# A power operation behind every second gather on GpSimd, from the eleventh row block to the end of a two-layer graph kernel

## The chip, the cores and the metric

The kernel runs on one core of a Trainium2 chip. The metric is the device time of one execution in microseconds, measured without a trace: the median of three runs. A traced execution of the same program gives the profile. In this text PE is TensorE, DVE is VectorE, ACT is ScalarE and POOL is GpSimd, as the profile names them.

## What is computed

The input is a node matrix `x` (2708 x 128, float32) and an adjacency matrix `adj` (2708 x 2708, float32), which is sparse: a row has its diagonal element and some neighbours, all with the same weight. Two layers follow each other. The first is a hyperbolic convolution with a dense product, the second a message layer whose inner sum runs over all pairs of nodes, but whose terms count only where `adj` isn't zero:

```python
# layer 0, in short: y from x and W, then
nominator = A_hat @ (gamma * XW)
denominator = _clamp_abs(A_hat @ (gamma - 1.0))
...
x = _layernorm(x + _L0_gnn_ref(x, adj, L0_gnn_W), axis=-1)
# layer 1
s = node_feats @ msg_w[:, :D].T
d = node_feats @ msg_w[:, D:].T
messages = gelu(s[:, None, :] + d[None, :, :] + msg_b)
aggregated = jnp.einsum('ijd,ij->id', messages, adj)
...
h = gelu(new_feats) + node_feats
x = _layernorm(x + layernorm(h) * ln_w + ln_b, axis=-1)
```

## The kernel before, in words

The 2708 rows are cut into 22 blocks of 128 (`NB`). For each block `b`, `layer0(b)` loads 1.4 MB of the transposed adjacency (`aT`, queue of SyncE), takes its sign on ScalarE (L364) and multiplies it with `y` on TensorE (L369). The same signs are used to find the edges: `keys` and `extract` encode the positions of nonzero elements, sort them with VectorE's top-8 instruction (L404) and place them, 128 edges to a tile, into 99 edge tiles for all blocks together. `TILES` gives the number of tiles of each of 25 lists; tile `t` belongs to one list and so to one block. For each tile there are `J[:, t]`, the column of each of its edges, and `F`, the flat address of the edge in `adj` (L500, L501).

GpSimd then runs two kinds of indirect DMA, both through the helper `gather` (L197):

- a V gather per tile, at the end of `extract`: it reads `adj` at the 128 addresses `F`. The values `V` are needed only in the check at the end (L848), which compares them with the weight of the row.
- a dd gather per tile, in `fetch`: it reads 128 rows of `table` (the product `d` of the second layer, written to memory by `layer0_end`, L583) at the rows `J`. The messages need these rows.

`fetch` issues up to four dd gathers, from block 14 on (`FETCH`) once per row block, later once in each call of `messages`, and fourteen times in a row at the end of layer 0. The rows go into a ring of `RING = 14` rooms of four tiles each. `messages` takes one room of up to four tiles: TensorE expands `s` for the edges (L736), VectorE builds the summing matrix `rv` (L738) and adds `dd` (L741), ScalarE takes the Gelu (L742), and TensorE sums over edges (L751). There are 26 such rooms: 24 of four tiles, one of two, one of one. When the last tile of a block is summed, `node` computes the update (L608 to L610) and the norms of its group (`finish`), and the result is stored.

GpSimd runs its instructions in the order in which they were issued, so V gathers, dd gathers and whatever else stands in its queue wait for one another. In `gather`, the argument `pause` puts a power operation on a tile of one column (`gap`, L202) into GpSimd's queue right behind the gather. It depends on nothing that changes and nothing reads its result. Before the change, V gathers of blocks below `PAUSED = 9` have it (61 of them) and no other gather.

Of the kernel before, what the change touches and what calls it, by code (L numbers as in the profile page):

```python
# [20 lines left out]
P = 128  # L21
# [7 lines left out]
CHUNKS = [(0, 10), (10, 20), (20, 22)]  # L29
PARTS = (0, 1, 2, 2)  # L30
GROUPS = [(0, 8), (8, 6), (14, 4), (18, 2), (20, 2)]
PAUSED = 9
EARLY = 8
FETCH = 14

# [3 lines left out]
SPLIT, BITS = 10, 16  # L39
# [42 lines left out]
def hyperbolic_then_message_kernel(  # L82
# [30 lines left out]
    w0_sb, wT, rowvec, o = pk[:, :D], pk[:, D : 5 * D].rearrange("p (i d) -> p i d", d=D), {}, 5 * D  # L113
# [55 lines left out]
    J = const.tile([P, NT], U32, name="J")  # L169
    V = const.tile([P, NT], F32, name="V")  # L170
# [25 lines left out]
    def gather(o, src, at, pause=False):  # L196
        last = nc.gpsimd.indirect_dma_start(  # L197
            out=o, out_offset=None, in_=src, in_offset=bass.IndirectOffsetOnAxis(ap=at, axis=0)
        )
        if pause:  # L200
            with tc.issue_after(last.ins), tc.high_priority():
                nc.gpsimd.tensor_tensor(gap, half, half, op=OP.pow)  # L202
# [10 lines left out]
    def flat(t):  # L213
        return t.rearrange("p b d -> p (b d)")
# [98 lines left out]
    for g, n in quads:  # L313
# [5 lines left out]
        t = small.tile([P, 4, D], F32, name="work", bufs=3)  # L319
        nc.vector.tensor_mul(t[:, :n, :], mx[:, g : g + n, :], mx[:, g : g + n, :])  # L320
        nc.vector.tensor_reduce(ss_m[:, g : g + n], t[:, :n, :], axis=AX.X, op=OP.add)
    for b in range(NB):
        t = small.tile([P, D], F32, name="junk")
# [89 lines left out]
    def extract(l):  # L413

        b, groups, c0, wa, wb, t0, n, late = LISTS[l]
# [34 lines left out]
        for k, _ in parts:  # L450
            first = n - late if k and wa else 0
            dl = deg[:, l, k + 1 : k + 2]
            for k0 in range(first, n, 4):
# [3 lines left out]
                o = flat(R[:, t0 + k0 : t0 + k1, :])  # L457
# [22 lines left out]
        F = small.tile([P, TMAX], U32, name="F", bufs=12)  # L480
        step = 512 // (C + 2)
        for k0 in range(0, n, step):
            k1 = min(n, k0 + step)
            w = k1 - k0
            t = slice(t0 + k0, t0 + k1)
# [16 lines left out]
                F[:, k0:k1], J[:, t], float(b * P * N - 1), rid[:, t], op0=OP.add, op1=OP.add  # L502
            )
        for t in range(t0, t0 + n):
            gather(V[:, t : t + 1], adj.rearrange("i (j o) -> (i j) o", o=1), F[:, t - t0 : t - t0 + 1], b < PAUSED)
        known[0] = b

    x1, x1T, gd = x_sb, xT, nom
# [183 lines left out]
    early, late, soon = {}, {}, set()  # L692
# [13 lines left out]
    rooms, sums, whole = [], {}, []  # L706
# [6 lines left out]
    def fetch():  # L713

        for _ in range(4):
            ready = [v for v in (True, False) if order[v] and order[v][0][0] < done[0] + RING]
            if not whole:
                ready = [v for v in ready if v and order[v][0][2] <= known[0]]
            if not ready:
                return  # L720
            q, k, _, t = order[min(ready, key=lambda v: order[v][0])].pop(0)
            while len(rooms) <= q:
                rooms.append(edge.tile([P, 4, P], F32, name="dd", bufs=RING))
            gather(rooms[q][:, k, :], table[: SPLIT * P] if t in soon else table, J[:, t : t + 1])

    def messages():

# [15 lines left out]
        for k, (b, t, first, final, before) in enumerate(ts):  # L743
# [12 lines left out]
            elif final:  # L756
                g0, gn = group[b]
                queue.append(node(gd[:, g0 : g0 + gn, :D], b - g0, b, g0, gn, [gd[:, b, :D]] if b < EARLY else []))
        fetch()
        step()  # L760
        step(1)
# [10 lines left out]
    with tc.issue_after(setup.ins):  # L772
        for b in range(NB):
            block = layer0(b)
            next(block)
            go_on(b, 0)
            for x in placed:
                next(x, None)
            placed = []
            next(block)  # L780
            go_on(b, 1)
            for x in found:
                next(x)
            placed, found = found, []
            sgn = next(block)
            for l in of_block[b]:
                keys(l, sgn)
                found.append(extract(l))
            if b == 0 or b == NB - 1:
                for x in found:  # L790
                    next(x)
                    next(x, None)
                for x in placed:
                    next(x, None)
                found, placed = [], []
            if b >= FETCH:
                fetch()
            for b0, b1 in CHUNKS:
                if b == b1 - 1 and b1 < NB:
                    ends.append((b1, layer0_end(b0, b1)))  # L800
                    next(ends[-1][1])
# [7 lines left out]
    for _ in range(RING):  # L809
        fetch()  # L810
# [25 lines left out]
    for i, v in enumerate(seconds):  # L836
        k = v.shape[1]
# [146 lines left out]
```

## Time and profile before

| | |
|---|---|
| time, median of 3 runs | 361.72 us (361.44 to 362.11) |
| traced execution | 472.48 us, span 470.8 us |
| gathers of either kind | 99 |
| power operations | 61, from 48.9 to 158.7 us |
| V gathers in the trace | first at 47.6 us, last at 310.0 us |
| dd gathers in the trace | first at 164.5 us, last at 403.2 us |

In the profile, a group's line gives source line, engine, operation, output and inputs, the count, then the busy time and the mean duration of one in ns, then the time that the engine was idle just before, and what ended most of that. A timeline's line gives start, length, engine, line and operation, and in brackets the idle time before it with what ended it. "remote", like "another core or an unknown queue", stands for a wait whose releaser isn't in the trace. "issue" is time in which the engine waited for nothing that the trace shows.

### The profile page before, as it was taken

To read this page: it belongs to the slowest core of one execution; us is meant where nothing else is said; L and a number is where in the kernel's file an instruction comes from. 1 tells how busy PE (TensorE), PEld (TensorE's weight loads), DVE (VectorE), ACT (ScalarE), POOL (GpSimd) and SP (SyncE) were. 2 spreads that over 40 slices of the span, in tenths; PEclk is the share of its full clock that TensorE was granted. 3 is DMA by queue.
4 is the path that set the end of the run, shared out by engine and by line. 5 is a ranking of instruction groups with operands and counts; after the bars stand their busy time and mean duration, and the time that the engine had idled before them with its cause. 6 is when DMAs were issued, how large, how long until landed. Compare 5 with 4: busy or idle time off the path is not lost.

```text
span 470.8 us, 8239 instructions
## 1 busy us (share of the span) xinstructions
PE 293.5 (62%) x2603; PEld 261.0 (55%) x2603; DVE 280.4 (60%) x1580; ACT 214.0 (45%) x609; POOL 242.4 (51%) x353
## 2 busy tenths in 40 slices
PE   4249999999999931252738947655300713999840
PEld 4139988999979820142627946544200712897730
DVE  0997998868979602022224779974000411799995
ACT  2953868786959802031324773932000201334441
POOL 6200888988888877735754400226776475200000
PEclk9758999999999965568957996859555665899865
DMA  8403544646644431122413300101211121100111
GB/s 335 207 1 124 194 179 135 236 142 230 222 172 158 161 117 37 28 79 95 151 28 141 126 1 24 34 11 45 52 50 50 30 54 36 24 1 4 43 37 43
DMA packets 16029, 45.15 MB, mean 96 GB/s; under 512 B 5418, under 2 KB 10942, under 8 KB 13166
## 3 DMA queue, kind: packets, MB, share of 16 engines
q1 hardware_dynamic: 9502, 37.43, 21.8%
q0 software_dynamic: 6336, 6.55, 5.6%
q10 hardware_dynamic: 144, 0.60, 0.4%
q8 instruction: 22, 0.36, 0.3%
q14 instruction: 25, 0.20, 0.1%
HBM read 41.74 MB, written 2.83 MB: 95 GB/s over the span
## 4 chain that ended last, share of the span: by engine, by line
PE 35%; DVE 27%; another core or an unknown queue 24%; ACT 6%; issue 5%; DMA 1%; DVEq 0%; ACTq 0%
PE mp L369 17%; PE kx L396 4%; PE mp L751 3%; DVE rv L738 2%; PE X L577 2%; DVE top L404 2%; PE sel L489 2%; DVE st L600 1%; PE X L736 1%; DMA xT<-in_x_t_dram 1%; DVE dd L741 1%; DVE nom L624 1%; PE kx L317 1%; PE sel L608 1%
## 5 line engine op out<-in xcount | busy, mean ns | idle before, releaser
L197 POOL DMA_INDIRECT V<-in_adj_dram,F x99 | 98.8, 998 | 108.5 <-DVE F L501 70.1
L369 PE MATMUL mp<-y,aT 128*128 128x130 f32 x968 | 141.7, 297 | 15.1 <-issue 14.8
L369 PEld LDWEIGHTS mp<-y,aT 128*128 128x128 f32 x968 | 127.1, 205 | 16.5 <-issue 16.3
L197 POOL DMA_INDIRECT dd<-table_dram,J x99 | 94.8, 958 | 47.8 <-issue 45.7
L364 ACT ACTIVATE sgn<-aT 128x2816 bf16<-128x2816 f32 x22 | 56.0, 2547 | 2.3 <-DMA aT<-in_adj_t_dram 2.1
L738 DVE TENSOR_SCALAR rv<-iotaN,rv_of 128x128 f32<-128x128 f32 x99 | 30.1, 347 | 42.8 <-PE X L736 34.2
L404 DVE MAX8 top<-kx 128x8 f32<-128x128 f32 (+3 forms) x133 | 25.3, 227 | 30.0 <-remote 25.4
L751 PE MATMUL mp<-rv,dd 128*128 128x128 f32 x198 | 35.7, 334 | 11.2 <-ACT dd L742 11.2
L489 PE MATMUL sel<-z,R 128*128 128x42 bf16 (+5 forms) x297 | 19.5, 194 | 31.6 <-issue 17.3
L202 POOL TENSOR_TENSOR gap<-gap 128x1 f32<-128x1 f32 x61 | 37.8, 620 | 1.5
L751 PEld LDWEIGHTS mp<-rv,dd 128*128 128x128 f32 x198 | 30.8, 236 | 13.4 <-ACT dd L742 12.1
L396 PE MATMUL kx<-kd,sgn 128*128 128x128 bf16 x484 | 32.9, 223 | 8.1 <-ACT sgn L364 8.1
L396 PEld LDWEIGHTS <-sgn 128*128 128x128 bf16 x484 | 28.1, 99 | 14.6 <-ACT sgn L364 8.5
L489 PEld LDWEIGHTS <-R 128*128 128x128 bf16 x297 | 15.2, 98 | 35.6 <-issue 19.6
L689 PE MATMUL mp<-ident,nom 128*128 128x128 f32 x44 | 10.0, 322 | 39.2 <-ACT nom L755 39.2
L494 DVE TENSOR_TENSOR work<-sel,place 128x120 f32<-128x120 f32 (+11 forms) x29 | 11.1, 382 | 37.4 <-remote 32.4
L742 ACT ACTIVATE dd<-dd 128x512 f32<-128x512 f32 (+2 forms) x26 | 15.8, 607 | 30.6 <-DVE dd L741 17.9
L456 ACT ACTIVATE away<-iota,mid 128x256 f16<-128x256 f32 (+3 forms) x54 | 28.7, 572 | 1.7 <-DVE mid L449 0.6
L689 PEld LDWEIGHTS mp<-ident,nom 128*128 128x128 f32 x44 | 7.1, 208 | 40.1 <-ACT nom L755 39.6
L736 PEld LDWEIGHTS <-R 128*128 128x128 bf16 x297 | 21.4, 108 | 12.4 <-issue 10.6
L755 ACT COPY nom<-mp 128x128 f32<-128x128 f32 x8 | 2.1, 262 | 46.8 <-remote 43.4
L408 ACT ACTIVATE junk_s<-kx 128x384 bf16<-128x384 f32 (+2 forms) x25 | 12.2, 486 | 18.2 <-DVE top L404 14.1
(224 smaller groups left out, 599.3 us busy)
## 6 DMA issues: line engine op xcount, KB each, us to landing
aT<-in_adj_t_dram SPq DMA_DIRECT2D x22, 1408.0 KB
V<-in_adj_dram,F POOLq DMA_INDIRECT x99
dd<-table_dram,J POOLq DMA_INDIRECT x99
xT<-in_x_t_dram SPq DMA_DIRECT2D x2, 704.0 KB
x_sb<-in_x_nm_dram SPq DMA_DIRECT2D x2, 704.0 KB
table_dram<-dt SPq DMA_DIRECT2D x4, 256.0 KB
out_dram<-nom SPq DMA_DIRECT2D x4, 256.0 KB
pk<-in_pack_dram ACTq DMA_DIRECT2D x1, 587.5 KB
```

The lines of the kernel that those rows point to most:

```text
L197: last = nc.gpsimd.indirect_dma_start(out=o, out_offset=None, in_=src, in_offset=bass.IndirectOffsetOnAxis(ap=at, axis=0))
L202: nc.gpsimd.tensor_tensor(gap, half, half, op=OP.pow)
L364: nc.scalar.activation(sgn, aT, AF.Sign, accum_out=signs[:, b : b + 1])
L369: p = nc.tensor.matmul(op[:, : D + 2], lhsT=aT[:, j, :], rhs=y[:, j, :], start=(j == 0), stop=(j == NB - 1))
L396: nc.tensor.matmul(kp[:, i * P : (i + 1) * P], lhsT=sgn[:, j, :], rhs=kd[:, q, :], start=False, stop=(i == len(groups) - 1 and j == j1 - 1),)
L404: nc.vector.max(top[:, c : c + 8], seg[:, s, :])
L456: nc.scalar.activation(r0, iota[:, k0 * P : k1 * P], AF.Abs, scale=2.0, bias=mid[:, k : k + 1])
L489: nc.tensor.matmul(sp[:, k, :], lhsT=R[:, t0 + k0 + k, :], rhs=z[:, i, :], start=(i == 0), stop=(i == 2))
L689: nc.tensor.matmul(ag[:, :P], lhsT=gd[:, b, :D], rhs=ident, start=True, stop=False)
L736: nc.tensor.matmul(X[:, k, :], lhsT=R[:, t, :], rhs=s3[:, b, i, :], start=(i == 0), stop=(i == 2))
L738: nc.vector.tensor_scalar(rv[:, k, :], iotaN, rid[:, t : t + 1], same[:, t : t + 1], op0=OP.is_equal, op1=OP.mult)
L751: nc.tensor.matmul(sums[b][:, :P], lhsT=dd[:, k, :], rhs=rv[:, k, :], start=(first and not mine), stop=final)
```

## The change

The power operation is to be spread over the rest of the gathers: all V gathers of blocks below 11 have it, from block 11 on every V gather of an odd tile, and of the dd gathers every one with odd `k`, the second and fourth of a room. It is for spacing the gathers that run back to back before the change, so that other engines have room between them.

```diff
-PAUSED = 9
 EARLY = 8
 FETCH = 14
...
         for t in range(t0, t0 + n):
-            gather(V[:, t : t + 1], adj.rearrange("i (j o) -> (i j) o", o=1), F[:, t - t0 : t - t0 + 1], b < PAUSED)
+            gather(V[:, t : t + 1], adj.rearrange("i (j o) -> (i j) o", o=1), F[:, t - t0 : t - t0 + 1], b < 11 or t % 2)
...
-            gather(rooms[q][:, k, :], table[: SPLIT * P] if t in soon else table, J[:, t : t + 1])
+            gather(rooms[q][:, k, :], table[: SPLIT * P] if t in soon else table, J[:, t : t + 1], k % 2)
```

## The prediction

> **What bounds the kernel now.** I read the times first, then the page's busy shares, its groups of instructions, then GpSimd's own timeline, the chain, and a table by stretch. The times already hold the main difficulty: 361.72 us is the median without a trace, while the traced execution took 472.48 us (span 470.8). The trace therefore holds about 110 us that the timed runs don't have, and the first job is to find which.
>
> ```profile
> PE 293.5 (62%) x2603; PEld 261.0 (55%) x2603; DVE 280.4 (60%) x1580; ACT 214.0 (45%) x609; POOL 242.4 (51%) x353
> PE 35%; DVE 27%; another core or an unknown queue 24%; ACT 6%; issue 5%; DMA 1%; DVEq 0%; ACTq 0%
> L197 POOL DMA_INDIRECT V<-in_adj_dram,F x99 | 98.8, 998 | 108.5 <-DVE F L501 70.1
> L197 POOL DMA_INDIRECT dd<-table_dram,J x99 | 94.8, 958 | 47.8 <-issue 45.7
> L202 POOL TENSOR_TENSOR gap<-gap 128x1 f32<-128x1 f32 x61 | 37.8, 620 | 1.5
> ```
>
> No engine is full, and 24% of the chain (113 us of 470.8) is a wait whose releaser the trace can't name. Without it the span would be 470.8 - 113 = 358 us, close to the untraced time. The stretches say where it sits (columns: window, length, then PE, PEld, DVE, ACT and POOL busy, clock, DMA share, GB/s):
>
> ```profile
> 125.00:150.00 25.00, 24.11 (x221) 21.25 (x219) 21.58 (x100) 19.52 (x55) 22.45 (x28) 1.00 0.50 169
> 180.00:200.00 20.00, 3.83 (x19) 2.85 (x19) 2.20 (x18) 3.04 (x11) 14.88 (x16) 0.50 0.11 30
> 340.00:360.00 20.00, 0.00 (x0) 0.00 (x0) 0.69 (x1) 0.00 (x0) 15.13 (x16) 0.50 0.20 52
> ```
>
> Up to 159 us every gather has its power operation and all engines are busy. After it gathers run back to back, and there the other engines nearly stop, while GpSimd goes on at an even beat. GpSimd's timeline at the border shows both beats:
>
> ```profile
> 157.66 0.99 POOL L197 DMA_INDIRECT V<-in_adj_dram,F  x1 [0.17 <-issue]
> 158.68 0.59 POOL L202 TENSOR_TENSOR gap<-gap 128x1 f32<-128x1 f32 x1
> 159.44 0.99 POOL L197 DMA_INDIRECT V<-in_adj_dram,F  x1 [0.17 <-DVE z L474]
> 160.74 0.96 POOL L197 DMA_INDIRECT V<-in_adj_dram,F  x1 [0.30 <-issue]
> 162.00 0.95 POOL L197 DMA_INDIRECT V<-in_adj_dram,F  x1 [0.30 <-issue]
> ...
> 360.44 0.95 POOL L197 DMA_INDIRECT dd<-table_dram,J  x1 [0.30 <-issue]
> 361.69 0.95 POOL L197 DMA_INDIRECT dd<-table_dram,J  x1 [0.30 <-issue]
> ```
>
> Start to start, a gather with its power operation takes 159.44 - 157.66 = 1.78 us, one without 162.00 - 160.74 = 1.26 us, and that 1.26 is the same at 361 us where nothing else runs. From 47.61 us (first gather) to 199.4 us GpSimd has no idle beyond these 0.2 to 0.3 us: it is behind with the V gathers and works off a queue.
>
> Now the timed run. If the unnamed waits are absent there, GpSimd's queue never empties: at 159.44 us it still has 38 V and 99 dd gathers, 137 in all, and 137 x 1.26 = 172.6 us, so the last gather ends at 332.0 us. Their inputs are in time: the row blocks pass at 7.35 us each (the sign activations before 159 us), so block 21's F would be there near 210 us, while the V gathers of blocks 17 to 21 stand behind 65 others in the queue (26 V, 39 dd) and come up at 241 us. After the last gather come its landing (2 us, below) and the last message with the final norms: from the last dd add at 448.34 us to the end at 470.77 that is 22.4 us. Sum 332.0 + 2 + 22.4 = 356.4, and 1.7 for what the time has over the span (472.48 - 470.8): 358.1 us. Measured is 361.72. So in the timed run I take the instruction stream of GpSimd as the path that sets the end, though the page shows it 51% busy. A second view agrees: with all data present, ten messages of four from 407.18 to 448.62 us (their Gelu starts) take 4.1 us each, and GpSimd delivers four gathers in 5.04 us, so the consumers wait for it.
>
> **What the Trainium skill says.** (1) Perfetto Trace Analysis, "GPSIMD Engine Instruction": reported spans of GpSimd are unreliable, and start-to-start spacing of consecutive instructions should be used. The trace agrees: a gather's span is 0.95 to 0.99 us, its spacing 1.26. (2) The same page, "DMA Instruction — SWDGE (GPSIMD)": the recorded end of such a gather is the end of descriptor writing, not of the data movement; so a gather occupies GpSimd for the whole 1.26 us, and landing comes on top. (3) DMA: Bandwidth & Descriptors, "Anatomy of one DMA — SWDGE (gpsimd) path", prices the fixed cost at about 2.0 us; the page's issue table gives no landing median for gathers, so I use it. (4) SBUF — State Buffer, "Who interferes with whom": a GpSimd instruction that reads SBUF and a VectorE one with two SBUF inputs hold a shared port in turn; TensorE and ScalarE wait for no one. The trace shows power operations stretched to 0.82 us at most (median 0.597), so this is small; and it can't explain the stops after 159 us, since TensorE and ScalarE stop too.
>
> **The change part by part.** The constant PAUSED goes: no cost. V gathers of blocks 9 and 10 (4 + 3) now all get the operation: 7 more. From block 11 on those with odd index (69 to 97): 15. Of the dd gathers those with k = 1 or 3: 24 full quads and one pair give 49. Together 71 power operations, 61 become 132. The order of the other four engines' instructions is unchanged; on GpSimd nine of the 71 end up behind another power operation instead of directly behind a gather, most in a row of seven just before the last 60 dd gathers.
>
> Price of one: 1.78 - 1.26 = 0.52 to 0.53 us between neighbours (0.59 to 0.60 of operation, the gap behind a gather 0.30 replaced by 0.03 + 0.17). Over the whole paused stretch (159.44 - 47.61) / 61 = 1.83 us a pair, so 0.57 with the stretched ones. Upper end: the longest operation, 0.82 + 0.17 - 0.27 = 0.72. I take 0.53, because the last 60 gathers run while VectorE is waiting, and little stretches them. 71 x 0.53 = 37.6 us (with 0.57: 40.5).
>
> What hides it? The operation reads and writes constants nobody waits for, but the gathers queued behind it wait, and behind those the dd adds (L741) and the last message. All 71 lie before the last gather. Were GpSimd ever idle in the timed run, that much would be hidden; my sum left 361.7 - 358.1 = 3.6 us unexplained, which is the most I find. So 361.7 + 37.6 = 399.3, less up to 3.6: 396 to 399, and I take 398. As a check, the floor by GpSimd alone is 332.0 + 37.6 + 2 + 22.4 + 1.7 = 395.7.
>
> **The rivals.**
> - Faster. The stops after 159 us exist in part in the timed run too, and the operation lets the other engines go on, as it does before 159 us. For it: the border is sharp, and no stop falls in the paused stretch. It needs gathers that cost less untraced, or GpSimd's floor forbids it. If the 0.30 us gap after a gather were only recording, a gather would cost 0.96: the last one before would end near 272 us, the run at 272 + 26 = 298, so 361.7 would hold 63 us of stops; after, the floor is 313 + 26 = 339 us. If the stops nearly vanish the time is about 345; if they only shrink with the count of gathers without the operation (137 to 66), 30 us stay and it is 369, slower again. Against it: the 1.26 sum meets 361.72 within 1%.
> - No change. GpSimd has slack in the timed run as in the trace (108.5 and 47.8 us idle before its gathers), the consumers set the end, and the operations fill that idle time: 361.7. Against it: those idle stretches follow the stops (6.9 us at 206, 29.5 at 300), and the consumers' 4.1 us per four is less than GpSimd's 5.04.
> - Partly hidden: GpSimd has about 15 to 20 us of slack, for instance waiting for the table's last rows before the final 60 dd gathers: 378 to 385.
> - Dearer: every operation at its stretched cost, 71 x 0.57 to 0.72: 402 to 413.
>
> **How the numbers follow.** Full cost on GpSimd's path (396 to 403) 0.60, dearer 0.04, partly hidden 0.11, no change 0.03, faster 0.22. Slower is 0.75, same 0.03, faster 0.22. The range starts at 354, which takes in no change and the near part of the faster case, and ends at 407, which takes in 0.57 with some to spare; outside stay about 0.16 of faster and 0.03 of dearer.
>
> **What would show it.** In the changed kernel's profile: 132 power operations; pairs at 1.78 and lone gathers at 1.26; the last dd gather about 38 us later than an unbroken queue would place it, with GpSimd's idle time before gathers nearly gone. I also expect the unnamed waits to shrink much, so that the traced span comes down towards the untraced time: if it falls while the untraced time rises, the stops belonged to tracing. I am wrong if gathers alternate in less than 3.04 us a pair (1.26 + 1.78), or if GpSimd has long idle times while VectorE or TensorE is full to the end, or if the untraced time falls below 361.

## The result, and the profile after

The changed kernel takes 400.24 us (median of 4 runs, 399.69 to 400.56), and the kernel before, run beside it, 361.92 us (361.44 to 363.2). The ratio is 1.1051, interval 1.1019 to 1.1083: 38.3 us slower. Ratios are taken from the fast runs alone, so a ratio can differ a little from the quotient of the two medians. The prediction was 398.0 us.

The page of the changed kernel: busy time of each engine, the chain by engine, the two kinds of gather and the power operation.

```profile
PE 282.8 (71%) x2603; PEld 255.0 (64%) x2603; DVE 281.3 (71%) x1580; ACT 213.2 (53%) x609; POOL 289.9 (73%) x424
PE 34%; DVE 22%; POOL 16%; DMA 12%; ACT 9%; issue 5%; DVEq 0%; POOLq 0%; ACTq 0%; SPq 0%
L196 POOL DMA_INDIRECT V<-in_adj_dram,F x99 | 100.1, 1012 | 52.0 <-DVE F L500 32.6
L196 POOL DMA_INDIRECT dd<-table_dram,J x99 | 97.2, 982 | 24.4 <-issue 22.1
L201 POOL TENSOR_TENSOR gap<-gap 128x1 f32<-128x1 f32 x132 | 81.6, 618 | 3.7
```

The 132 power operations are there. The wait on an unnamed releaser, 24% of the chain before, is gone from it, and GpSimd, which the chain before did not hold at all, has 16%. The traced execution took 400.42 us (span 398.7) and is one of the four runs behind the median, so the page shows what was timed. For the kernel before it took 472.48 us, far outside its runs.

GpSimd's timeline at the end of the gathers:

```profile
364.94 0.94 POOL L196 DMA_INDIRECT dd<-table_dram,J  x1 [0.30 <-issue]
365.91 0.58 POOL L201 TENSOR_TENSOR gap<-gap 128x1 f32<-128x1 f32 x1
366.67 0.99 POOL L196 DMA_INDIRECT dd<-table_dram,J  x1 [0.17 <-ACT agT L661]
367.97 0.95 POOL L196 DMA_INDIRECT dd<-table_dram,J  x1 [0.30 <-issue]
...
372.89 1.00 POOL L196 DMA_INDIRECT dd<-table_dram,J  x1 [0.17 <-issue]
```

Two gathers and one operation take 367.97 - 364.94 = 3.03 us start to start, against 1.78 + 1.26 = 3.04 before. The last gather ends at 373.89. From 159.97 us to there lie 137 gathers and 71 operations, and no idle time over 0.5 us between two of them.

The stretches (columns: window, length, PE, PEld, DVE, ACT and POOL busy, clock, DMA share, GB/s):

```profile
180.00:200.00 20.00, 20.00 (x225) 19.03 (x225) 16.21 (x111) 12.80 (x38) 15.75 (x19) 1.00 0.65 222
...
250.00:275.00 25.00, 3.77 (x47) 3.57 (x45) 0.69 (x1) 1.75 (x5) 21.13 (x28) 0.63 0.04 8
275.00:300.00 25.00, 15.51 (x135) 14.78 (x135) 13.11 (x43) 5.49 (x14) 20.91 (x27) 0.70 0.12 30
```

From 180 to 200 us, where the trace of before had TensorE busy for 3.83 of 20 us, it is full now. This is not yet the work of the operations: `e6_none` below has none and is full there too. From 250 to 275 us VectorE is busy for 0.69 us while GpSimd runs: there the others wait for the queue. VectorE stands in line behind the check of V, which needs the last V gather:

```profile
L847 DVE TENSOR_TENSOR work<-V,rv_of 128x99 f32<-128x99 f32 x1 | 0.3, 266 | 28.7 <-DMA V<-in_adj_dram,F 28.7
```

That wait of 28.7 us should cost little by itself, because the dd gathers that the messages need stand behind the same V gathers in GpSimd's queue; no run isolates it.

### The profile page after: what moved, and what is told of

It reads as the page before. It is cut to its first block, busy times and chain, and to the rows that moved or that the text cites. A ratio compares the mean times of both kernels' runs of the same rounds, so it can differ in the third digit from the quotient of the medians.

```text
span 398.7 us, 8310 instructions
## 1 busy us (share of the span) xinstructions
PE 282.8 (71%) x2603; PEld 255.0 (64%) x2603; DVE 281.3 (71%) x1580; ACT 213.2 (53%) x609; POOL 289.9 (73%) x424
## 4 chain that ended last, share of the span: by engine, by line
PE 34%; DVE 22%; POOL 16%; DMA 12%; ACT 9%; issue 5%; DVEq 0%; POOLq 0%; ACTq 0%; SPq 0%
PE mp L368 17%; POOL dd L196 8%; DMA aT<-in_adj_t_dram 8%; POOL gap L201 4%; PE kx L395 4%; POOL V L196 3%; DMA dd<-table_dram,J 3%; ACT sgn L363 3%; PE X L576 3%; PE sel L488 2%; PE mp L750 2%; DMA xT<-in_x_t_dram 1%; ACT nom L639 1%; PE kx L316 1%; DVE dd L740 1%
## 5 line engine op out<-in xcount | busy, mean ns | idle before, releaser
L196 POOL DMA_INDIRECT V<-in_adj_dram,F x99 | 100.1, 1012 | 52.0 <-DVE F L500 32.6
L368 PE MATMUL mp<-y,aT 128*128 128x130 f32 x968 | 128.9, 284 | 0.5 <-DMA aT<-in_adj_t_dram 0.5
L368 PEld LDWEIGHTS mp<-y,aT 128*128 128x128 f32 x968 | 117.6, 194 | 1.5 <-DMA aT<-in_adj_t_dram 0.8
L196 POOL DMA_INDIRECT dd<-table_dram,J x99 | 97.2, 982 | 24.4 <-issue 22.1
L201 POOL TENSOR_TENSOR gap<-gap 128x1 f32<-128x1 f32 x132 | 81.6, 618 | 3.7
L750 PE MATMUL mp<-rv,dd 128*128 128x128 f32 x198 | 37.9, 348 | 17.2 <-ACT dd L741 17.2
L750 PEld LDWEIGHTS mp<-rv,dd 128*128 128x128 f32 x198 | 32.4, 246 | 20.2 <-ACT dd L741 19.6
L735 PE MATMUL X<-s,R 128*128 128x128 bf16 x198 | 18.1, 240 | 30.1 <-DVE dd L740 30.1
L740 DVE TENSOR_TENSOR dd<-X,dd 128x512 f32<-128x512 f32 (+1 forms) x17 | 11.4, 671 | 19.0 <-DMA dd<-table_dram,J 18.8
L847 DVE TENSOR_TENSOR work<-V,rv_of 128x99 f32<-128x99 f32 x1 | 0.3, 266 | 28.7 <-DMA V<-in_adj_dram,F 28.7
L605 PE MATMUL sel<-pk,xT 128*128 128x128 f32 x44 | 11.7, 355 | 5.9 <-ACT nom L609 5.4
```

The costliest lines, as they stand in the source:

```text
L196: last = nc.gpsimd.indirect_dma_start(out=o, out_offset=None, in_=src, in_offset=bass.IndirectOffsetOnAxis(ap=at, axis=0))
L368: p = nc.tensor.matmul(op[:, : D + 2], lhsT=aT[:, j, :], rhs=y[:, j, :], start=(j == 0), stop=(j == NB - 1))
L735: nc.tensor.matmul(X[:, k, :], lhsT=R[:, t, :], rhs=s3[:, b, i, :], start=(i == 0), stop=(i == 2))
L750: nc.tensor.matmul(sums[b][:, :P], lhsT=dd[:, k, :], rhs=rv[:, k, :], start=(first and not mine), stop=final)
```

## The experiments

Two theories stood against each other. The queue: GpSimd's instruction stream sets the end, an operation costs about 0.53 us wherever it stands behind a gather after 159 us, and the stops in the trace of before belong to tracing. The stops: they are in the timed runs too, and operations between the gathers shrink them.

The runs fell on four chips, here A to D. The kernel before took 478.67 us on A (472.85 to 483.02), 363.49 on B, 363.01 on C and 363.25 on D. The lowest of its 23 times on A is as long as the traced 472.48 us, so on chip A the timed runs were as slow as the trace of before. Each result below is read against the kernel before on its own chip. Every chip was measured at one time only, so where a chip is named, a state that it was in at that time would fit as well. The chip of the first trace is not on record. In the experiments the traced execution is always one of the timed runs.

### No operation, on chip A and on chip B

`e1_none` and `e6_none` are one program, without any of the 61 operations that the kernel before has:

```diff
-gather(V[:, t : t + 1], ..., F[:, t - t0 : t - t0 + 1], b < PAUSED)
+gather(V[:, t : t + 1], ..., F[:, t - t0 : t - t0 + 1], False)
```

> No gather has a power operation: 61 fewer than before. Theory (GpSimd's queue sets the end, each operation costs it about 0.53 us, the stops belong to tracing): 32 us less on GpSimd up to 159 us, but in the changed kernel's trace the last rows of the table are stored only near 248 us, and the last 57 to 60 dd gathers need them: 248 + 60 x 1.26 + 26 + 2 = 352 us, so 345 to 352, faster than before; the traced span stays far above the time. Rival (in timed runs too, gathers that run back to back stop the other engines, and the operation relieves them): slower than before, 365 us or more.

On chip A: 514.39 us, ratio 1.0821 (1.0733 to 1.0908). It has fewer instructions on GpSimd and takes 36 us more. The rival had the direction, from a starting point of 362 us that did not hold on this chip.

> No power operation at all, as e1, for the other condition of the chip if this comparison lands in it. Where before is near 362: 345 to 352 by theory A (GpSimd's time is the path and the operations only cost). Where before is near 478: 514 as before.

On chip B: 355.2 us, ratio 0.9711 (0.9643 to 0.9779). It is faster, but by less than the 345 to 352 us expected. The chain by engine and one stretch, first for chip A, then for chip B, there with the stretch from 180 to 200 us as well:

```profile
PE 28%; another core or an unknown queue 28%; DVE 24%; issue 8%; ACT 7%; DMA 3%; POOL 0%; DVEq 0%; ACTq 0%; POOLq 0%; SPq 0%
200.00:220.00 20.00, 4.56 (x37) 3.92 (x35) 1.41 (x9) 2.18 (x5) 15.12 (x17) 0.74 0.21 66
```

```profile
PE 44%; DVE 24%; DMA 18%; ACT 7%; POOL 3%; issue 3%; DVEq 0%; POOLq 0%; SPq 0%; ACTq 0%
180.00:200.00 20.00, 20.00 (x217) 19.03 (x214) 15.67 (x103) 13.87 (x45) 15.31 (x16) 1.00 0.68 243
200.00:225.00 25.00, 16.52 (x132) 13.63 (x131) 23.17 (x143) 16.07 (x38) 19.21 (x20) 0.86 0.18 46
```

In these stretches the same program runs its gathers back to back on both chips. On A the other engines stop beside them (VectorE 1.41 of 20 us), on B they don't (23.17 of 25 us), and both runs were traced. So the trace does not make the stops, and gathers without an operation do not bring them on every chip.

The second reading is of size: 61 x 0.53 = 32 us were taken out on chip B and only 8.3 us came back. GpSimd's timeline there says why:

```profile
149.72 0.94 POOL L197 DMA_INDIRECT V<-in_adj_dram,F  x1 [23.53 <-DVE F L501]
...
157.38 0.97 POOL L197 DMA_INDIRECT dd<-table_dram,J  x1 [2.93 <-DMA table_dram<-dt]
158.65 0.94 POOL L197 DMA_INDIRECT V<-in_adj_dram,F  x1 [0.30 <-DVE top L404]
```

Without operations GpSimd catches up with VectorE, waits 23.53 us for addresses, then 2.93 us for the table. That makes 26.5 of the 32 us, so before about 157 us most of the operations' time is paid from this idle time, and only what comes after it counts in full. From 157.38 to 327.02 us there are 133 gathers and no further wait, 1.275 us each on the mean.

### Each half alone, on chip A

`e2_v_only` gives the V gathers their added operations and leaves the dd gathers without; `e3_dd_only` does the reverse.

```diff
 # e2_v_only: in the V gather
-b < PAUSED
+b < 11 or t % 2
 # e3_dd_only: in the dd gather
-J[:, t : t + 1])
+J[:, t : t + 1], k % 2)
```

> Only the V half of the change: 22 more operations than before, all ahead of the last 60 dd gathers. Theory: 22 x 0.53 = 11.7 us, so 373 to 374. If GpSimd waits for the table there and hides them: 362 to 365. If the dd half alone costs: 362.

> Only the dd half of the change: 49 more operations than before. Theory: 49 x 0.53 = 26 us, so 388; with e2 it sums to the 38.3 us of the whole change. If the dd gathers had slack behind the messages: well under 380.

Both forecasts start from 362 us for the kernel before, which did not hold on this chip. Measured beside 478.67 us: the V half 469.06 us, ratio 0.9865 (0.9779 to 0.9952); the dd half 435.97 us, ratio 0.9188 (0.9099 to 0.9277). Behind 0, 61, 83 and 110 of the 198 gathers the operation gives 514.39, 478.67, 469.06 and 435.97 us: on this chip the time falls with the count. The verdict on `e1_none` and on both halves is unclear: the runs of the kernel before spread over 10 us there. Still, the 36 us of `e1_none` and the 43 us of the dd half lie far outside that, the 9.6 us of the V half do not, so its gain is weak. The stretches, first for the V half, then for the dd half:

```profile
160.00:180.00 20.00, 19.82 (x224) 18.17 (x223) 14.86 (x90) 17.18 (x49) 16.86 (x20) 1.00 0.51 170
180.00:200.00 20.00, 6.70 (x38) 4.90 (x37) 3.17 (x22) 2.67 (x13) 15.90 (x18) 0.61 0.29 98
...
330.00:360.00 30.00, 5.31 (x29) 4.63 (x27) 1.81 (x5) 0.80 (x2) 22.68 (x25) 0.50 0.23 52
```

```profile
160.00:180.00 20.00, 10.22 (x93) 8.44 (x93) 6.43 (x42) 7.57 (x24) 15.87 (x19) 0.77 0.30 95
180.00:200.00 20.00, 7.61 (x51) 6.35 (x51) 3.17 (x15) 4.46 (x10) 16.15 (x19) 0.63 0.11 27
...
330.00:360.00 30.00, 21.38 (x175) 18.56 (x173) 17.35 (x61) 8.00 (x24) 24.98 (x30) 0.89 0.20 44
```

Each half relieves its own stretch. Operations in the V stretch push the first stop back: TensorE is busy for 19.82 of 20 us from 160 to 180 us, against 10.22. Operations among the dd gathers keep the end alive: 21.38 of 30 us from 330 to 360 us, against 5.31, while GpSimd is busy alike (24.98 and 22.68). Between 180 and 200 us both are stopped.

### Operations where there is nothing to space

`e4_early45` takes the kernel before and puts 45 operations into GpSimd's idle time ahead of the first gather.

```diff
+for _ in range(45):
+    nc.gpsimd.tensor_tensor(gap, half, half, op=OP.pow)
```

> The kernel before with 45 more power operations, all on GpSimd ahead of its first gather, where it waits idle from 15 to 47 us; 45 x 0.63 = 28 us fit in. Theory (only GpSimd's time on the path counts): 362, no change. Rival (an operation costs the run by itself[...]): 362 + 45 x 0.53 = 386, or some part of it.

On chip A: 476.13 us, ratio 0.9964 (0.9929 to 0.9998). The 45 operations are 27.2 us of work on GpSimd, and the time is at most 0.7% lower. It is not the number of operations that counts but their place, on this chip for the relief and, by `e6_none`, on chip B for the cost.

### The changed kernel again, on chips B, C and D

> The changed kernel, run beside the kernel before wherever this lands. In the last comparison the kernel before took 478.7 us instead of 362, so the stops were in its timed runs. Theory A (two conditions of the chip: without stops GpSimd's queue sets the end, with stops gathers without an operation halt the other engines): where before is near 362, this is 400; where before is near 478, this is 400 to 430, faster than before, since it has 66 gathers without the operation and e3, with 88, took 436. Theory B (the cost of the operations adds to whatever before takes): 38 us more than before in either condition.

> The changed kernel again, beside the kernel before. On the first chip tried (before at 478.7 us) e3, with 88 gathers without the operation, took 436; on the second (before at 363.5) this took 401.5. Theory A (a chip either has stops or not; stops come with gathers without the operation): with before near 478 this is 400 to 430, so faster; with before near 362 it is 400 to 402. Theory B (38 us on top of before in either condition): 516 or 400.

> The changed kernel again. Beside a kernel before of some 363 us: 400 to 402. Beside a kernel before of some 478 us: theory (the operation keeps the gathers apart, and the halts shrink by more than it costs) 400 to 430, faster than before by a tenth; rival (the cost adds up in either condition) 505 to 515.

401.52 us on B, ratio 1.1038 (1.0985 to 1.1091); 401.55 on C, 1.1076 (1.1044 to 1.1108); 400.48 on D, 1.1049 (1.1006 to 1.1093). The result repeats on every chip where the kernel before takes some 363 us. No run of the changed kernel fell on chip A, so the other half of these expectations, 400 to 430 us against 505 to 516 among the stops, was not tried.

### The price of an operation, on chips B and C

`e8_pow_all` puts the operation behind all 198 gathers, `e7_memset_all` a memset of the same column in its place, and `e10_dd_only` is the program of `e3_dd_only`.

```diff
 # e8_pow_all and e7_memset_all: in both gathers
+True
 # e7_memset_all
-nc.gpsimd.tensor_tensor(gap, half, half, op=OP.pow)
+nc.gpsimd.memset(gap, 0.5)
```

> Every one of the 198 gathers has the power operation: 137 more than before. Theory A: GpSimd's queue alone, 362 + 137 x 0.53 = 434 to 438 us, and no stops in either condition, as before 159 us. If stops stay in spite of the spacing: well above 440.

> Every one of the 198 gathers is followed by a memset of one column instead of a power operation on some of them. In the traces a memset of one column takes a step of 0.03 us, so the spacing of gathers should stay near 1.26 us. If the time between gathers is what matters: like no operation at all (e6: 514, or 345 to 352 without stops). If any instruction between two gathers lets the others go on: no stops, and 345 to 365 in either condition.

> The dd half of the change alone, as e3, which so far was seen only beside a kernel before at 478.7 us. Theory A: 49 x 0.53 = 26 us over before where before is near 362, so 388; 436 where before is near 478. If some of the 49 operations fall into time in which GpSimd waits anyway: under 385 in the first case.

All 198: 436.81 us, ratio 1.2006 (1.1949 to 1.2064). Against the kernel before these are 137 more, and (436.81 - 363.49) / 137 = 0.535 us each. The dd half: 387.53 us, ratio 1.0685 (1.0652 to 1.0719), so 24.5 us for 49, 0.50 each. Both meet what was expected. The V half, by difference from the changed kernel on the same chip: 401.55 - 387.53 = 14.0 us for 22, 0.64 each. In the two traced executions the last gathers end at 372.64 and 360.81 us, 11.8 us apart, which is only 0.54 each; so it is not shown that an operation costs more among the V gathers. The memset: 358.55 us, ratio 0.9882 (0.9856 to 0.9909). GpSimd's timeline with the memset:

```profile
301.17 0.12 POOL L202 MEMSET gap<- 128x1 f32 x1
301.48 1.12 POOL L197 DMA_INDIRECT dd<-table_dram,J  x1 [0.19 <-issue]
302.59 0.12 POOL L202 MEMSET gap<- 128x1 f32 x1
302.90 1.00 POOL L197 DMA_INDIRECT dd<-table_dram,J  x1 [0.19 <-issue]
303.90 0.12 POOL L202 MEMSET gap<- 128x1 f32 x1
304.21 0.94 POOL L197 DMA_INDIRECT dd<-table_dram,J  x1 [0.19 <-issue]
305.15 0.12 POOL L202 MEMSET gap<- 128x1 f32 x1
305.46 0.94 POOL L197 DMA_INDIRECT dd<-table_dram,J  x1 [0.19 <-issue]
```

Memset and gather together step by 1.25 to 1.42 us: 0.12 of memset and 0.19 behind it take the place of the 0.30 gap that a lone gather has. Against no operation at all on the same chip the 198 memsets cost 358.55 - 355.2 = 3.4 us, 0.02 each, and the runs of either program spread over 5 to 7 us. So it is hardly the count of instructions on GpSimd that costs; it is the 0.6 us length of the power operation. What the expectation asked for, whether any instruction between two gathers relieves the stops, a chip without stops can't answer.

### A version that should beat both

`e11_v_last` has no operation, and moves the last twelve V gathers, which only the check needs, behind the last dd gather. With them the part of the check that reads V moves behind the last messages in the program.

```diff
-gather(V[:, t : t + 1], ..., F[:, t - t0 : t - t0 + 1], b < PAUSED)
+if b < BACK:
+    gather(V[:, t : t + 1], ..., F[:, t - t0 : t - t0 + 1])
+else:
+    back.append((t, F, t - t0))
...
+while done[0] < len(work):
+    messages()
+with tc.issue_after(newest[0].ins):
+    for t, F, k in back:
+        gather(V[:, t : t + 1], ..., F[:, k : k + 1])
+while queue:
+    step()
```

> No operation behind any gather, and the twelve V gathers of the blocks from the seventeenth on moved behind the last dd gather on GpSimd, so that the dd gathers, which the aggregation waits for, come up to 12 x 1.26 = 15 us earlier. Theory (the place of an instruction in GpSimd's order decides, not the number of instructions): beside a kernel before of some 363 us, where the same kernel without the move took 355, it takes 342 to 350: the last dd gather ends 10 to 15 us earlier and part is given back where VectorE's check of V waits in its queue. Rival (the table's last store or the other engines set the end by then, or the wait of the check moves into the tail): 353 to 362. Beside a kernel before of some 478 us it shows the halts again and takes 480 or more.

On chip D: 363.13 us, ratio 1.0 (0.9978 to 1.0021). The theory's 342 to 350 us were not reached; it came out a little above the rival's range. GpSimd's timeline:

```profile
231.99 0.94 POOL L197 DMA_INDIRECT dd<-table_dram,J  x1 [0.30 <-issue]
249.26 0.94 POOL L197 DMA_INDIRECT dd<-table_dram,J  x1 [16.32 <-issue]
...
323.37 1.07 POOL L197 DMA_INDIRECT dd<-table_dram,J  x1 [0.30 <-issue]
324.74 1.03 POOL L197 DMA_INDIRECT V<-in_adj_dram,F  x1 [0.30 <-issue]
...
338.62 0.94 POOL L197 DMA_INDIRECT V<-in_adj_dram,F  x1 [0.30 <-issue]
```

The dd gathers left over read the whole table, whose last store is issued at 246.6 us, so the 15 us taken out came back as an idle time of 16.32 us. The trace itself names no cause for this wait. In `e6_none` the same V gathers ran from 236 to 251 us: they had filled a wait. The last dd gather ends at 324.4 us, only 2.6 us earlier than the 327.0 there, and then the check waits for V:

```profile
341.24 0.26 DVE L860 TENSOR_TENSOR work<-V,rv_of 128x99 f32<-128x99 f32 x1 [10.23 <-DMA V<-in_adj_dram,F]
```

The fastest programs seen where the kernel before takes 363 us are `e6_none` and `e7_memset_all`, both on chip B; on chip A the first of them is the slowest, and the second was not run there.

## Why the prediction was right, step by step

**The path.** That GpSimd's queue sets the end held: no idle time over 0.5 us between gathers from 159.97 us to the last one, the added operations paid in full, and the other engines waiting near 260 us. The sum for the kernel before put the last gather's end at 332.0 us with 1.26 us for a gather. `e6_none` gives 1.275 on the mean, so as an estimate 137 of them from 159.44 us take 174.7 us and end at 334.1 us; with the changed kernel's tail of 398.7 - 373.89 = 24.8 us and 1.7 this is 360.6, against 361.92 measured. So of the 3.6 us that the prediction left unexplained, and offered as room to hide operations, some 2.1 are the gathers' longer mean step. No trace shows the kernel before without the stops, so this stays an estimate.

The prediction's second view misread its lines, against its own case: from 407.18 to 448.62 us the trace of before has twelve messages of four, not ten, so 3.45 us each instead of 4.1. The consumers are faster still beside the 5.04 us of four gathers.

**The count and the price.** 71 operations are right, as is the row of seven ahead of the last dd gathers:

```profile
278.10 4.43 POOL L201 TENSOR_TENSOR gap<-gap 128x1 f32<-128x1 f32 x7
```

The price of 0.53 us is met by `e8_pow_all` (0.535) and by the result, 38.3 / 71 = 0.54. It is a mean: 0.50 in the dd half, 0.54 to 0.64 in the V half, where these seven stand behind one another at 4.43 / 7 = 0.63 each.

**The landing and the tail.** Taken at 2.0 us from the Trainium skill (DMA: Bandwidth & Descriptors, "Anatomy of one DMA — SWDGE (gpsimd) path"). The changed kernel's chain shows 2.50 from a gather's start to its landing, and the measurement decides (columns: start, length, step):

```profile
364.94 2.50 DMA dd<-table_dram,J
367.47 0.69 DVE dd L740
...
373.70 0.69 DVE dd L740
...
376.16 0.26 DVE dd L740
```

The prediction set its 2.0 us behind the gather's whole step, 1.26 + 2.0 = 3.26 us after the start, so the term was some 0.8 us too long all the same. The chain also leaves GpSimd before the last gather: from the landing of the gather at 364.94 us VectorE goes on to 393.6 us with no idle time over 0.24 us, and the rows of the five gathers behind it are there when it comes to them. From the last gather's end to the end of the span are 24.8 us, against the prediction's 2 + 22.4 = 24.4; the sum came out, by a slightly different path.

**The stops.** The prediction took the stops for a thing of tracing, and gave as its sign that the traced span falls while the untraced time rises. Both happened, and the conclusion is wrong all the same. On chip A the traced executions show the stops and are as slow as the other timed runs, and all 23 times of the kernel before are long; on B, C and D no chain of a traced run has an unnamed wait, with or without operations. The page before and the times before were measured under two different conditions. Comparing the trace with the untraced time still gave the right path for the timed runs. That the changed kernel was then timed without the stops too was luck: beside stops the halves of the change came out faster, not slower.

**The rivals.** The faster one was told with "the stops exist in the timed run too". On chip A they do, and there the halves of the change gain 1.4% (weak) and 8.1%. Where the result was measured they don't, so nothing stood against the cost. No change and partly hidden fall by the unbroken queue after 159.97 us. Hidden operations do exist, but before 157 us: 61 of them cost 8.3 us there instead of 32.

**What stays open.** What makes the other engines stop beside unspaced gathers on one chip and not on three, and what the whole change does there. The two halves, at 469.06 and 435.97 us, suggest a gain; it wasn't run. The trace of before gives one hint: within a stop TensorE still works off products one by one, 2.80 us apart, and between them it waits for nothing that the trace shows.

```profile
194.01 0.38 PE L369 MATMUL mp<-y,aT 128*128 128x130 f32 x1 [2.43 <-issue]
196.81 0.37 PE L369 MATMUL mp<-y,aT 128*128 128x130 f32 x1 [2.42 <-issue]
```

So at least there the stop is not a wait for a tile or a transfer that the trace names. Whether the chip or something else that ran at that time makes the difference was not tried.

## What to carry to other kernels

Where one engine's in-order queue never runs dry, each instruction put into it costs what it adds to the step, start to start, whether anybody reads its result or not; while the queue still waits for its inputs the same instruction costs little or nothing, so ask first where the queue stops waiting. When a trace is far longer than the timed runs, do not put the difference down to tracing: run the kernel before again, traced and untraced, before a theory is built on it. And when work is moved out of the way, look for what it was covering: twelve gathers taken from the path uncovered a wait of about the same length.

## What the runs showed of the hardware

The same program took 355.2 us on one chip and 514.39 us on another, each measured at one time. On the second, TensorE, VectorE and ScalarE nearly stop beside back-to-back indirect gathers on GpSimd, while GpSimd keeps its own step (a mean of 1.26 us between neighbouring gathers there, 1.28 on the first). There a 0.6 us operation between gathers helps (478.67 to 435.97 us with 49 among the dd gathers), while on the others it costs 0.50 to 0.64 us. A memset of 0.12 us behind a gather hides almost wholly in the gap of 0.30 us that the gather leaves anyway.
